# A gated recurrence on the matrix engine: from 64x64 tiles to 64x32 tiles

## The chip, the cores and the metric

The kernel runs as one program on one core of a Trainium2 chip. The metric is device time in microseconds, the median of a few executions. Beside these times there is one profiled execution, whose trace the views below are read from. Engines are named as the profile names them: PE is the matrix engine and PEld its weight loads, DVE, ACT and POOL are the vector, scalar and GpSimd engines, SP is the engine that only issues DMAs here. All data are float32.

## What is computed

The input is `x[8, 32, 256, 256]` (batch, channel, row, column). Four layers follow one another, each adding its result to its input: a Fourier layer, a 5x5 convolution, a gated recurrence over the image's columns, and running maxima in four directions with a 1x1 mix. Only the recurrence is changed. With a column of 256 rows x 32 channels as its state, it is, for each batch and each of 255 columns in turn (cut from the reference):

```
pad = jnp.pad(prev_col, ((0, 0), (1, 1), (0, 0)))
x = jnp.concatenate([pad[:, :-2], pad[:, 1:-1], pad[:, 2:]], axis=-1)
i_vals = jnp.einsum('bhk,ok->bho', x, weight_ih) + bias_ih
h_vals = jnp.einsum('bhc,oc->bho', cur_col, weight_hh) + bias_hh
...
r = jax.nn.sigmoid(r_i + r_h)
z = jax.nn.sigmoid(z_i + z_h)
n = jnp.tanh(n_i + r * n_h)
return n * z + cur_col * (1.0 - z)
```

So each gate (r, z, n) needs three taps of the previous column (the row above, the same row, the row below; 32 channels each) and, called "own" in the kernel, one product of the current input column. For r and z the own part is added into the same sum; for n it stays apart (`nh`), since it is multiplied by r first.

## The kernel before, in words

**Layout.** The 128 partitions hold 4 row classes x 32 channels: partition 32 i + c has the rows h = 4 q + i, and q (64 of them) lies along the free axis. A state tile is `hs[P, 4 batches, 64 + 2]`, with a zero at either end. Two neighbouring classes, 0 and 1 or 2 and 3, form a half ("pair") of 64 partitions. Row h's neighbours are in the classes beside it: for classes 0 and 3 one neighbour lies in the other half and at q - 1 or q + 1.

**Order of the work.** The batch is cut in two chains x = 0 and 1 of four batches each, which take turns: half step n = 2 w + x does column w for chain x. There are 510 half steps with products. Each needs the state of half step n - 2. The order is written out by hand (a manual schedule), every engine takes its instructions in program order.

**Products** (`gates`, `own`, `within`, `across`; lines 736 to 795). A weight tile of 64x64 holds the two classes of one half. `within` (L742) is two matmuls, half to the same half: for a gate it covers the same-row tap and the neighbour inside the half, and with other weights the own part. `across` (L750) is two matmuls from one half to the other, once for the neighbour at the same q (`SAME`) and once for the one at q - 1 or q + 1 (`NEXT`). A half step is so 3 gates x (2 + 2 + 2) plus 3 own x 2 = 24 matmuls of 256 columns each. `gates` writes out their order: r within, z across, ni within, z across, r own of the *next* half step, r across, z within, r across, z own of the next, ni across, nh own of the next, ni across. Explicit waits on a semaphore `tiles` keep matmuls that add into one PSUM tile from different halves apart. PSUM has eight tiles: r, z, nh and ni for either chain.

**Elementwise part** (`step`, L817 to L832). ACT: sigmoid of r (L817), sigmoid of -z (L819) and of z (L820), tanh (L824), and then one piece of `normalise` (L722), which prepares the columns of the next block of eight columns. DVE: (nh + bias) * r (L818), + ni (L823), one piece of other work, * z (L829), + a (L831), which gives the new state. POOL: a = (1 - z) * column (L826) and the residual add (L832). The pieces on DVE are the running maximum (L853) in the half steps of chain 0 and statistics (L864) in those of chain 1.

**Blocks and queues.** A block is eight columns. The input columns `xw` are loaded on SP two blocks ahead (L711); their normalised form `norms[bi]` is one tile per block, two of them in turn, filled a half block of one batch at a time by `normalise`. SP also stores the sums and the running maxima of a block (L842), 16 DMAs of 256 KB each.

Of the kernel before, what the change touches and what calls it, by code (L numbers as in the profile page):

```python
# [9 lines left out]
F32 = mybir.dt.float32  # L10
AF = mybir.ActivationFunctionType
# [5 lines left out]
P = 128  # L17
B, C, H, W = 8, 32, 256, 256
# [5 lines left out]
A = 4  # L24
Q = H // A
# [267 lines left out]
def flat(t):  # L293
    return t.rearrange("p b w q -> p b (w q)")
# [377 lines left out]
def recurrence(tc, k, d, x2d, x3d, fwd, stb, first, loaded, mean1, mv3):  # L672
# [7 lines left out]
    NH = 4  # L680
    NC = 2
    BC = B // NC
    with ExitStack() as ctx:
        one = ctx.enter_context(tc.tile_pool(name="bc", bufs=1))
        blk = ctx.enter_context(tc.tile_pool(name="bb", bufs=2))
# [3 lines left out]
        def rows(i):  # L689
            return slice(32 * i, 32 * i + 32)  # L690
# [12 lines left out]
            nc.vector.memset(t, 0.0)  # L703
        bst = one.tile([P, B, NB, 6], F32, name="bst")

        raws, norms, psums = {}, {}, {}

        def load(bi):
            if bi:
                t = blk.tile([P, B, WB, Q], F32, name=f"xw_{bi}", tag="xw", bufs=4)  # L710
                nc.sync.dma_start(  # L711
                    out=flat(t), in_=x2d[:, :, :, bi * WB : (bi + 1) * WB, :].rearrange("b a c w q -> (a c) b (w q)")
                )
            else:
                t = first
                nc.sync.dma_start(out=flat(t[:, B - 1 : B]), in_=first_columns(x2d, B - 1, B))
            raws[bi] = t
            norms[bi] = blk.tile([P, B, WB, Q], F32, name=f"xn_{bi}", tag="xn")

        def normalise(bi, b, half):  # L720
            w = slice(half * WB // 2, (half + 1) * WB // 2)
            nc.scalar.activation(  # L722
                norms[bi][:, b, w], raws[bi][:, b, w], AF.Identity, bias=shift[:, b : b + 1], scale=sc[:, 1, b : b + 1]
            )

        R, Z, N = 0, 1, 2
        OWN, WITHIN, SAME, NEXT = 1, 0, 2, 3
        pairs = (slice(0, 64), slice(64, 128))


        sem, count = tc.alloc_semaphore("tiles"), [0]
# [8 lines left out]
        def within(out, kind, gate, src, start, stop, wait=None):  # L740
            for i, r in enumerate(pairs):
                ins = nc.tensor.matmul(out[r], lhsT=weights[r, kind, gate, :], rhs=src[r], start=start, stop=stop)  # L742
                if wait and i == 0:
                    ins._wait_ge(sem, wait)

        def across(out, kind, gate, prev, stop, wait=None, signal=False):
            for i, q0 in ((0, 2), (1, 0)):
                r = pairs[i]
                q0 = q0 if kind == NEXT else 1
                ins = nc.tensor.matmul(  # L750
                    out[pairs[1 - i]],
                    lhsT=weights[r, kind, gate, :],
                    rhs=prev[r, :, q0 : q0 + Q],
                    start=False,
                    stop=stop,
                )
                if wait and i == 0:
                    ins._wait_ge(sem, wait)
                if signal and i == 1:
                    ins.then_inc(sem, 1)  # L760
                    count[0] += 1
                    tc.add_to_no_dep_group("signals", ins.ins)
                    tc.no_tile_sem_insts.add(ins.ins.name)
                    some[0] = True

        def own(n, gate):
# [5 lines left out]
            out = psums[n, key] = ps.tile([P, BC, Q], F32, name=f"{key}_{n}", tag=f"{key}{x}")  # L772
            within(out, OWN, gate, norms[w // WB][:, x * BC : (x + 1) * BC, w % WB, :], True, gate == N)

        def gates(n, prev):

            same = prev[:, :, 1 : 1 + Q]
# [12 lines left out]
            across(ni, SAME, N, prev, False, signal=True)  # L792
            own(n + 1, N)
            across(ni, NEXT, N, prev, True)

        def step(w, x):
            bi, wi = w // WB, w % WB
            bs = slice(x * BC, (x + 1) * BC)
            raw, cur = raws[bi][:, bs, wi, :], norms[bi][:, bs, wi, :]
            new = hs[x][w % NH][:, :, 1 : 1 + Q]  # L800
            if w == 0:
                nc.vector.tensor_copy(new, cur)
            else:
                n, prev = NC * w + x, hs[x][(w - 1) % NH]
                if n == NC:
                    for gate in (Z, R, N):
                        own(n, gate)
                    nc.tensor.drain().then_inc(sem, 1)
                    count[0] += 1
# [7 lines left out]
                rs = nc.scalar.activation(r, p["r"], AF.Sigmoid, bias=brz[:, 0:1])  # L817
                nc.vector.scalar_tensor_tensor(m, p["nh"], bhh[:, 2:3], r, ALU.add, ALU.mult)  # L818
# [4 lines left out]
                nc.vector.tensor_tensor(m, p["ni"], m, ALU.add)  # L823
# [5 lines left out]
                ins = nc.vector.tensor_tensor(m, m, z, ALU.mult)  # L829
                tc.add_manual_dep(ins.ins, product.ins.name, AFTER, reason="the sum behind it then need not wait")  # L830
                free(nc.vector.tensor_tensor(new, m, a, ALU.add))  # L831
            nc.gpsimd.tensor_tensor(raw, raw, new, ALU.add)  # L832
# [14 lines left out]
        def running(bi, wi):  # L847
            def piece():
                if wi == 0:
                    tops[bi] = blk.tile([P, B, WB, Q], F32, name=f"fm_{bi}", tag="fm", bufs=2)  # L850
                t, x = tops[bi], raws[bi][:, :, wi]
                last = t[:, :, wi - 1] if wi else tops[bi - 1][:, :, WB - 1] if bi else x
                nc.vector.tensor_tensor(t[:, :, wi], x, last, ALU.max)  # L853
                if wi == WB - 1:
                    store(bi, fwd, t)

            pieces[0].append(piece)
# [323 lines left out]
```

## Time and profile before

| what | value |
|---|---|
| time, median of 3 runs (range) | 3231.57 us (3227.11 to 3237.39) |
| profiled execution, first to last instruction | 3226.3 us |
| granted PE clock, mean over the span | 0.931 |
| PE busy, whole span | 2866.3 us (89%) |
| recurrence, 1160 to 2530 us: PE, DVE, ACT, POOL busy | 1356.41, 1230.82, 1129.28, 705.79 us |
| PE clock granted in the recurrence | 1.00 |

The page gives no time of the profiled execution other than its span; 3226.3 us is 5.3 us, or 0.16%, under the median. A row of groups reads: line, engine, operation, output<-inputs, shapes, count | busy us in all, mean ns of one | idle us of the engine just before them, with what ended it. A float32 matmul appears as two weight loads and two matmul records, called passes below. The recorded end of a matmul is modelled; its start is not, and so spacing is read from starts.

### The profile page before, as it was taken

How to read it: one execution, taken by the hardware profiler on the slowest of the kernel's cores; microseconds unless marked ns; L12 is line 12 of the kernel's file. 1: busy time of each engine (PE TensorE's matmuls, PEld its weight loads, DVE VectorE, ACT ScalarE, POOL GpSimd, SP SyncE). 2: the span in 40 equal slices, each digit the busy share in tenths (PEclk: the TensorE clock that was granted, in tenths of full speed). 3: DMA queues.
4: the chain of work that ended last, by engine and by line, in shares of the span. 5: the costliest groups of instructions: out<-in, count | busy, mean ns of one | idle time of the engine just before them, and what ended most of it. 6: DMA issues, size and time to landing. Idle time of an engine off the chain costs nothing.

```text
span 3226.3 us, 112014 instructions
## 1 busy us (share of the span) xinstructions
PE 2866.3 (89%) x47802; PEld 1666.4 (52%) x47802; DVE 2614.3 (81%) x5188; ACT 1862.5 (58%) x4362; POOL 860.8 (27%) x1241
## 2 busy tenths in 40 slices
PE   7975799999999969999999999999999577777776
PEld 4655344444444446666666666666666233333332
DVE  5742577777767759999999999999999799999998
ACT  3422365565565657888888888888887222222222
POOL 0110011111111145555555555555555200000000
PEclk9985899999999989999999999999999788888998
DMA  9978577888777545665555555666554588878885
GB/s 385 387 288 193 129 187 193 196 194 195 186 182 197 138 110 153 159 159 151 146 148 147 147 146 151 157 159 159 155 143 121 188 306 305 308 311 314 313 308 217
DMA packets 527058, 655.75 MB, mean 203 GB/s; under 512 B 388825, under 2 KB 389737, under 8 KB 500829
## 3 DMA queue, kind: packets, MB, share of 16 engines
q1 hardware_dynamic: 483628, 494.33, 53.9%
q0 software_dynamic: 17200, 85.05, 8.1%
q10 hardware_dynamic: 25728, 69.21, 5.4%
q8 instruction: 374, 6.13, 0.8%
q14 instruction: 128, 1.04, 0.1%
HBM read 371.63 MB, written 272.63 MB: 200 GB/s over the span
## 4 chain that ended last, share of the span: by engine, by line
PE 54%; DVE 25%; DMA 8%; SPq 6%; issue 5%; ACT 2%; POOL 0%; DVEq 0%; ACTq 0%; POOLq 0%
PE r L742 13%; PE z L742 12%; PE ni L742 6%; PE nh L742 6%; DMA x2d<-x 6%; SPq L547 5%; DVE rv L993 5%; PE vp L490 4%; DVE x L527 3%; PE yp L131 3%; DVE dq L1005 2%; DVE m L1009 2%; DVE m L1007 2%; DVE x L1002 2%; DVE m L1008 2%
## 5 line engine op out<-in xcount | busy, mean ns | idle before, releaser
L750 PE MATMUL z<-hs,weights 64*64 64x256 f32 x4080 | 539.4, 382 | 0.0
L750 PE MATMUL r<-hs,weights 64*64 64x256 f32 x4080 | 525.2, 375 | 0.0
L750 PE MATMUL ni<-hs,weights 64*64 64x256 f32 x4080 | 524.9, 375 | 0.0
L832 POOL TENSOR_TENSOR xw<-xw,hs 128x256 f32<-128x256 f32 x496 | 339.5, 684 | 635.6 <-DVE hs L831 635.6
L527 DVE SCALAR_TENSOR_TENSOR x<-vp,r,x 64x512 f32<-64x512 f32 (+2 forms) x640 | 350.8, 563 | 164.6 <-PE vp L490 137.8
L1039 ACT ACTIVATE ot<-o,bres 128x512 f32<-128x512 f32 x256 | 155.4, 690 | 541.5 <-PE o L1023 533.9
L490 PE MATMUL vp<-x,c_conv 64*64 64x384 f32 (+2 forms) x4608 | 457.5, 514 | 0.2
L826 POOL TENSOR_TENSOR a<-zm,xn 128x256 f32<-128x256 f32 x510 | 372.7, 731 | 6.4 <-issue 6.2
L1023 PE MATMUL o<-m,wsc 32*32 32x512 f32 x3072 | 237.1, 830 | 152.9 <-DVE m L1009 106.3
L824 ACT ACTIVATE n<-n,bih 128x256 f32<-128x256 f32 x510 | 260.8, 511 | 184.4 <-DVE n L823 184.4
L490 PEld LDWEIGHTS vp<-x,c_conv 64*64 64x64 f32 x4608 | 238.3, 138 | 234.5 <-issue 128.5
L742 PE MATMUL z<-xn,weights 64*64 64x256 f32 x2040 | 305.3, 376 | 24.2 <-ACT xn L722 24.2
L742 PE MATMUL r<-hs,weights 64*64 64x256 f32 x2040 | 319.0, 389 | 4.4 <-DVE hs L831 3.4
L742 PE MATMUL r<-xn,weights 64*64 64x256 f32 x2040 | 305.6, 376 | 1.0 <-ACT rs L817 1.0
L742 PE MATMUL nh<-xn,weights 64*64 64x256 f32 x2040 | 305.7, 376 | 0.0
L742 PE MATMUL z<-hs,weights 64*64 64x256 f32 x2040 | 305.2, 376 | 0.0
L742 PE MATMUL ni<-hs,weights 64*64 64x256 f32 x2040 | 305.2, 375 | 0.0
L722 ACT ACTIVATE xn<-xw,shift,turned 128x256 f32<-128x256 f32 x496 | 291.9, 589 | 0.0
L750 PEld LDWEIGHTS ni<-hs,weights 64*64 64x64 f32 x4080 | 284.4, 133 | 0.3
L818 DVE SCALAR_TENSOR_TENSOR n<-nh,bhh,rs 128x256 f32<-128x256 f32 x510 | 246.3, 483 | 45.3 <-ACT rs L817 30.7
L750 PEld LDWEIGHTS r<-hs,weights 64*64 64x64 f32 x4080 | 281.1, 131 | 0.2
L817 ACT ACTIVATE rs<-r,brz 128x256 f32<-128x256 f32 x510 | 242.7, 476 | 50.8 <-PE r L750 30.3
(165 smaller groups left out, 6267.2 us busy)
## 6 DMA issues: line engine op xcount, KB each, us to landing
xb<-in_xl_dram POOLq DMA_DIRECT2D x96, 768.0 KB, 6.4
xa<-in_xt_dram SPq DMA_DIRECT2D x64, 1024.0 KB
x<-x3d SPq DMA_DIRECT2D x32, 2048.0 KB
fw<-fwd SPq DMA_DIRECT2D x32, 2048.0 KB
out_dram<-ot ACTq DMA_DIRECT2D x64, 1024.0 KB
xw<-x2d SPq DMA_DIRECT2D x31, 2048.0 KB
fwd<-fm SPq DMA_DIRECT2D x248, 256.0 KB
x3d<-xw SPq DMA_DIRECT2D x248, 256.0 KB
```

The source lines that it names most:

```text
L490: ins = nc.tensor.matmul(vps[bank][to], lhsT=k.conv[r, P : P + 64] if kind == 2 else k.conv[r, o], rhs=pair_of(u, ch, g, lo, hi, (2, 0)[i] ...
L527: nc.vector.scalar_tensor_tensor(x, src[o], r1[rows, g : g + 1], x, ALU.mult, ALU.add, accum_out=s1[rows, 0, n, ch, g : g + 1])
L547: (nc.gpsimd if 2 * u + ch == 2 * n - 1 and p % 2 else nc.sync).dma_start(out=x2d[b, a, c0 : c0 + CH, TS * t + lo : TS * t + hi].rearrange ...
L722: nc.scalar.activation(norms[bi][:, b, w], raws[bi][:, b, w], AF.Identity, bias=shift[:, b : b + 1], scale=sc[:, 1, b : b + 1])
L742: ins = nc.tensor.matmul(out[r], lhsT=weights[r, kind, gate, :], rhs=src[r], start=start, stop=stop)
L750: ins = nc.tensor.matmul(out[pairs[1 - i]], lhsT=weights[r, kind, gate, :], rhs=prev[r, :, q0 : q0 + Q], start=False, stop=stop,)
L817: rs = nc.scalar.activation(r, p["r"], AF.Sigmoid, bias=brz[:, 0:1])
L818: nc.vector.scalar_tensor_tensor(m, p["nh"], bhh[:, 2:3], r, ALU.add, ALU.mult)
L824: nc.scalar.activation(m, m, AF.Tanh, bias=bih[:, 2:3])
L826: product = nc.gpsimd.tensor_tensor(a, zm, cur, ALU.mult)
L832: nc.gpsimd.tensor_tensor(raw, raw, new, ALU.add)
L1023: nc.tensor.matmul(pts[b2][i][32 * j : 32 * j + 32].rearrange("p (w q) -> p w q", q=Q), lhsT=wsc[q, b2, t, :], rhs=src[j][q, b2], start=first,
```

## The change

All products of the recurrence are made in tiles of 64 input partitions x 32 output partitions. For a gate there are two kinds left, each of four matmuls, one for each output class: `near` takes the class's own half (same-row tap and neighbour in the half), `far` takes the other half (for classes 0 and 3 the neighbour at q - 1 or q + 1, for 1 and 2 the one at the same q), with the weights that were there before, cut to 32 output columns. The own parts of r and z are near tiles. The own part of nh is made in far tiles, from `swapped`, a copy of the normalised columns with the two halves of partitions exchanged, and it is issued in two parts of two batches (128 columns) each. A new function `swap` makes the copy with two DMAs on SP for each half block. The normalised columns become one tile for each half block (three in turn) in place of one for a block (two in turn). A drain of PE ahead of the first half step is dropped.

```
-            norms[bi] = blk.tile([P, B, WB, Q], F32, name=f"xn_{bi}", tag="xn")
...
+            if b == 0:
+                norms[bi, half] = blk.tile([P, B, HB, Q], F32, name=f"xn_{bi}_{half}", tag="xn", bufs=3)
...
+        def swap(bi, half):
+
+            t = swapped[bi, half] = blk.tile([P, B, HB, Q], F32, name=f"xs_{bi}_{half}", tag="xs")
+            for i in range(2):
+                nc.sync.dma_start(out=flat(t[pairs[1 - i]]), in_=flat(norms[bi, half][pairs[i]]))
...
+        FAR = ((NEXT, 0), (SAME, 1), (SAME, 1), (NEXT, 2))
+
+        def tiles(out, gate, operand, other, start, stop, cols=slice(0, BC), wait=None, signal=False):
...
+            for j in range(A):
+                r = pairs[1 - j // 2 if other else j // 2]
+                kind, src = operand(j)
+                ins = nc.tensor.matmul(
+                    out[rows(j), cols],
+                    lhsT=weights[r, kind, gate, rows(j % 2)],
+                    rhs=src[r, cols],
+                    start=start,
+                    stop=stop,
+                )
+                if wait is not None and j == 0:
                     ins._wait_ge(sem, wait)
...
+            src = column(swapped if gate == N else norms, w, x)
+            tiles(psums[n, key], gate, lambda j: (OWN, src), gate == N, True, gate == N, cols)
...
-            within(r, WITHIN, R, same, False, False)
-            across(z, SAME, Z, prev, False, wait=count[0], signal=True)
-            first = count[0]
-            within(ni, WITHIN, N, same, True, False)
-            across(z, NEXT, Z, prev, False, signal=True)
+            first = near(r, R, prev, start=False, stop=False, signal=True)
+            second = far(ni, N, prev, start=True, stop=False, signal=True)
+            third = near(z, Z, prev, start=False, stop=False, signal=True)
+            own(n + 1, N, slice(0, BC // 2))
+            far(r, R, prev, start=False, stop=True, wait=first)
             own(n + 1, R)
-            across(r, SAME, R, prev, False, wait=first)
-            within(z, WITHIN, Z, same, False, True, wait=count[0])
-            across(r, NEXT, R, prev, True)
+            own(n + 1, N, slice(BC // 2, BC))
+            near(ni, N, prev, start=False, stop=True, wait=second)
+            far(z, Z, prev, start=False, stop=True, wait=third)
             own(n + 1, Z)
-            across(ni, SAME, N, prev, False, signal=True)
-            own(n + 1, N)
-            across(ni, NEXT, N, prev, True)
...
-                    nc.tensor.drain().then_inc(sem, 1)
-                    count[0] += 1
...
                 for b in range(B):
                     normalise(0, b, half)
+                swap(0, half)
...
                             normalise(bi + 1, b, half)
+                            if b == B - 1:
+                                swap(bi + 1, half)
```

More of the change, by code (lines that the diff above doesn't have):

```diff
@@ L682, in recurrence @@
     BC = B // NC
+    HB = WB // 2
     with ExitStack() as ctx:
@@ L704, in recurrence @@
         bst = one.tile([P, B, NB, 6], F32, name="bst")
-        raws, norms, psums = {}, {}, {}
+        pairs = (slice(0, 64), slice(64, 128))
+        raws, norms, swapped, psums = {}, {}, {}, {}
         def load(bi):
@@ L717, in load, with column @@
             raws[bi] = t
-            norms[bi] = blk.tile([P, B, WB, Q], F32, name=f"xn_{bi}", tag="xn")
         def normalise(bi, b, half):
-            w = slice(half * WB // 2, (half + 1) * WB // 2)
+            w = slice(half * HB, (half + 1) * HB)
+            if b == 0:
+                norms[bi, half] = blk.tile([P, B, HB, Q], F32, name=f"xn_{bi}_{half}", tag="xn", bufs=3)
             nc.scalar.activation(
-                norms[bi][:, b, w], raws[bi][:, b, w], AF.Identity, bias=shift[:, b : b + 1], scale=sc[:, 1, b : b + 1]
-            )
+                norms[bi, half][:, b],
+                raws[bi][:, b, w],
+                AF.Identity,
+                bias=shift[:, b : b + 1],
+                scale=sc[:, 1, b : b + 1],
+            )
+        def swap(bi, half):
+            t = swapped[bi, half] = blk.tile([P, B, HB, Q], F32, name=f"xs_{bi}_{half}", tag="xs")
+            for i in range(2):
+                nc.sync.dma_start(out=flat(t[pairs[1 - i]]), in_=flat(norms[bi, half][pairs[i]]))
+        def column(t, w, x):
+            return t[w // WB, w % WB // HB][:, x * BC : (x + 1) * BC, w % HB, :]
         R, Z, N = 0, 1, 2
         OWN, WITHIN, SAME, NEXT = 1, 0, 2, 3
-        pairs = (slice(0, 64), slice(64, 128))
         sem, count = tc.alloc_semaphore("tiles"), [0]
@@ L737, in free @@
                 tc.declare_no_dep(ins.ins, group="signals", reason="later matmuls of the same half step end last")
[L740 to L749, printed above, removed]
+        FAR = ((NEXT, 0), (SAME, 1), (SAME, 1), (NEXT, 2))
@@ L750, in across @@
+        def tiles(out, gate, operand, other, start, stop, cols=slice(0, BC), wait=None, signal=False):
+            for j in range(A):
+                r = pairs[1 - j // 2 if other else j // 2]
+                kind, src = operand(j)
                 ins = nc.tensor.matmul(
[L751 to L754, printed above, removed]
+                    out[rows(j), cols],
+                    lhsT=weights[r, kind, gate, rows(j % 2)],
+                    rhs=src[r, cols],
+                    start=start,
@@ L755, in across @@
                     stop=stop,
                 )
-                if wait and i == 0:
+                if wait is not None and j == 0:
                     ins._wait_ge(sem, wait)
-                if signal and i == 1:
-                    ins.then_inc(sem, 1)
-                    count[0] += 1
[L762 to L766, printed above, removed]
+            if signal:
+                ins.then_inc(sem, 1)
+                count[0] += 1
+                tc.add_to_no_dep_group("signals", ins.ins)
+                tc.no_tile_sem_insts.add(ins.ins.name)
+                some[0] = True
@@ L768, in own, with near, far, operand @@
+            return count[0]
+        def near(out, gate, prev, **flags):
+            return tiles(out, gate, lambda j: (WITHIN, prev[:, :, 1 : 1 + Q]), False, **flags)
+        def far(out, gate, prev, **flags):
+            def operand(j):
+                kind, q0 = FAR[j]
+                return kind, prev[:, :, q0 : q0 + Q]
+            return tiles(out, gate, operand, True, **flags)
+        def own(n, gate, cols=slice(0, BC)):
             w, x = divmod(n, NC)
@@ L771, in own @@
             key = ("r", "z", "nh")[gate]
-            out = psums[n, key] = ps.tile([P, BC, Q], F32, name=f"{key}_{n}", tag=f"{key}{x}")
-            within(out, OWN, gate, norms[w // WB][:, x * BC : (x + 1) * BC, w % WB, :], True, gate == N)
+            if (n, key) not in psums:
+                psums[n, key] = ps.tile([P, BC, Q], F32, name=f"{key}_{n}", tag=f"{key}{x}")
+            src = column(swapped if gate == N else norms, w, x)
+            tiles(psums[n, key], gate, lambda j: (OWN, src), gate == N, True, gate == N, cols)
         def gates(n, prev):
-            same = prev[:, :, 1 : 1 + Q]
             r, z = psums[n, "r"], psums[n, "z"]
             ni = psums[n, "ni"] = ps.tile([P, BC, Q], F32, name=f"ni_{n}", tag=f"ni{n % NC}")
-            within(r, WITHIN, R, same, False, False)
-            across(z, SAME, Z, prev, False, wait=count[0], signal=True)
-            first = count[0]
-            within(ni, WITHIN, N, same, True, False)
-            across(z, NEXT, Z, prev, False, signal=True)
+            first = near(r, R, prev, start=False, stop=False, signal=True)
[3 more added lines that the diff above has]
+            far(r, R, prev, start=False, stop=True, wait=first)
             own(n + 1, R)
-            across(r, SAME, R, prev, False, wait=first)
-            within(z, WITHIN, Z, same, False, True, wait=count[0])
-            across(r, NEXT, R, prev, True)
+            own(n + 1, N, slice(BC // 2, BC))
+            near(ni, N, prev, start=False, stop=True, wait=second)
+            far(z, Z, prev, start=False, stop=True, wait=third)
             own(n + 1, Z)
-            across(ni, SAME, N, prev, False, signal=True)
-            own(n + 1, N)
-            across(ni, NEXT, N, prev, True)
         def step(w, x):
@@ L798, in step @@
             bs = slice(x * BC, (x + 1) * BC)
-            raw, cur = raws[bi][:, bs, wi, :], norms[bi][:, bs, wi, :]
+            raw, cur = raws[bi][:, bs, wi, :], column(norms, w, x)
             new = hs[x][w % NH][:, :, 1 : 1 + Q]
@@ L807, in step @@
                         own(n, gate)
-                    nc.tensor.drain().then_inc(sem, 1)
-                    count[0] += 1
                 gates(n, prev)
```

## Prediction, made before the changed kernel was run

> **What bounds the kernel now.** I read the sums by stretch first, to see the stage the change is in; then that stage's waits; then its timeline. The stretch holding the recurrence (columns: length; busy us and count of PE, PEld, DVE, ACT, POOL; clock; DMA share; GB/s):
>
> ```profile
> 1160.00:2530.00 1370.00, 1356.41 (x24480) 921.81 (x24480) 1230.82 (x2568) 1129.28 (x2552) 705.79 (x1029) 1.00 0.56 146
> ```
>
> PE is busy nearly throughout at full clock, DVE nine tenths. A half step's length comes from the first and last start of a line that runs once in each:
>
> ```profile
> L818 DVE SCALAR_TENSOR_TENSOR n<-nh,bhh,rs x510: 461/483/488, 1170.1 to 2523.0; 128x256 f32<-128x256 f32 x170
> ```
>
> (2523.0 - 1170.1) / 509 = **2.658 us**. PE has 24 matmuls of two passes on four tiles, 12 passes per tile. Their starts in the trace lie 0.2157 us apart: 12 x 0.2157 = 2.588. So PE stands still for 0.07 us in a half step. The stage's waits (waiter <- whom: us, times, longest) say on what:
>
> ```profile
> PEld r L742 <- DVE hs L831: 110.6, 363, 2.3
> DVE n L818 <- ACT rs L817: 30.7, 130, 6.5
> ACT rs L817 <- PE r L750: 29.8, 141, 0.7
> ```
>
> This is a ring: PE waits for the state, ACT for r, DVE for ACT. PE is the tightest part of it, but how near is the next? DVE over two half steps (start, length):
>
> ```profile
> 1600.18 0.48 DVE L818 SCALAR_TENSOR_TENSOR n<-nh,bhh,rs 128x256 f32<-128x256 f32 x1
> 1600.77 0.42 DVE L823 TENSOR_TENSOR n<-ni,n 128x256 f32<-128x256 f32 x1
> 1601.11 0.68 DVE L864 BATCH_NORM_STATS2 bst<-xw 128x6 f32<-128x512 f32 x1
> 1601.84 0.43 DVE L829 TENSOR_TENSOR n<-n,zs 128x256 f32<-128x256 f32 x1
> 1602.30 0.42 DVE L831 TENSOR_TENSOR hs<-n,a 128x256 f32<-128x256 f32 x1
> 1602.91 0.48 DVE L818 SCALAR_TENSOR_TENSOR n<-nh,bhh,rs 128x256 f32<-128x256 f32 x1 [0.19 <-ACT rs L817]
> 1603.50 0.42 DVE L823 TENSOR_TENSOR n<-ni,n 128x256 f32<-128x256 f32 x1
> 1603.84 0.89 DVE L853 TENSOR_TENSOR fm<-xw,fm 128x512 f32<-128x512 f32 x1
> 1604.65 0.41 DVE L829 TENSOR_TENSOR n<-n,zs 128x256 f32<-128x256 f32 x1
> 1605.10 0.42 DVE L831 TENSOR_TENSOR hs<-n,a 128x256 f32<-128x256 f32 x1
> ```
>
> Read the starts. In the lower half step DVE never pauses: the maximum (L853) fills the time until L829. In the upper one it waits for tanh and, at its end, for r. DVE is the near second.
>
> **What the Trainium skill says.** TensorEngine Tiling (Array Packing), Tiling Modes: 64x32 gives eight independent tiles, 64x64 four. The trace agrees, in another stage with exactly these tiles and float32, at twice the columns (start, length):
>
> ```profile
> 335.87 1.95 PE L424 MATMUL up<-tt,c_gw 64*32 64x512 f32 x32
> ```
>
> The 32 passes start in four groups of eight; within a group 7 ns apart, groups 429 ns apart when running. Eight tiles are truly at work, each at 2 x 214.5 ns for twice the columns. PSUM — Partial Sum Buffer, PSUM bank collisions: two row tiles may not write one bank and quadrant at once. Hence the waits of far on near; no trace shows a collision. TensorE: Matmul & The Clock Gate, HAM oscillation: long idle gaps (over some 3.4 us) lower the clock. The trace agrees so far: a stretch with PE busy 12.68 of 17.00 us (2805 to 2822) was still granted 1.00.
>
> **The change, part by part.**
>
> *Products.* Near tiles: r, ni, z and two own parts, 5 matmuls or 10 passes each. Far tiles: ni, r, z and nh, 4 matmuls, 8 passes' worth. At 0.2157 us the longer queue is **10 x 0.2157 = 2.16 us** in place of 2.59. Can a pass hold 0.2157 with 256 columns? Weight loads must hide behind it. A row half now loads 4 x 32 columns in a pass, before 2 x 64: the same. And L131 (128x32 tiles, 256 columns, four loads of the same rows per pass) starts its groups 216 ns apart. A first group of L424 was followed 24 ns late (453 for 429), so I bound the pass at 0.214 to 0.240 (0.216 + 0.024) and take 0.216. Issuing 160 PE instructions a half step doesn't limit either, since the 32x32 stage (L1023) starts a load, a matmul and another load every 16.7 ns (5.6 ns each, 0.89 us for 160).
>
> The two 128-column parts of nh have passes of 107 ns, about one weight load (L424: 103 to 106 ns recorded), so they may take up to some 30 ns more each, 4 x 0.03 = 0.12 us. At 0 or at 0.12 they lie in the far tiles' spare 2 x 0.216 = 0.43 us.
>
> *When each sum is ready*, from the first near r: near r and far ni end at 0.43; half of nh at 0.65; far r waits for near r's signal. PE's end to the start of the waiting sigmoid is 0.3 us in the trace (r's last pass ends at 1.78, L817 starts at 2.05 to 2.09), so far r starts at 0.65 to 0.75, ends by 1.2: **sigmoid of r at 1.5 in place of 2.07**. Behind the waiting far r stand own r and all that follows; near tiles are busy with near z until 0.86, so at most its issue is delayed. Near ni and far z end by 1.8 to 2.0; their waits are long satisfied. z's sigmoid then comes 0.4 to 0.6 us behind r's where it was 0.37 behind; the start of a (L826) is what could feel it.
>
> *The same chain's ring*: state to PE 0.06, PE 1.5, sigmoid to the end of L831 3.07 to 3.17 (L817 starts at 2.05 and 2.09, L831 ends at 5.12 and 5.26): 4.68 us for two half steps, 2.34 each. So neither PE (2.16) nor this ring (2.34) binds; DVE and ACT are late next.
>
> *DVE's ring*, by smallest spacings of starts. L818 to L823 0.59. L823 to L829: 1.07 with statistics (tanh 0.46 later, 0.51 long, 0.10 to react), 1.18 mean with the maximum (mean 908 ns). L829 to L831 0.45, L831 to the next L818 0.34. Sums: **2.46 and 2.56, mean 2.51**. ACT's ring, with the sigmoid of r behind `normalise`: L817 to L818 0.51, to L823 0.59, to tanh 0.46, to L722 0.42, to the next L817 0.49, sum 2.47. POOL: state of n - 1 to a 0.71, a 0.73, reaction 0.11: 1.55 to L829, where DVE needs about 1.58; it fits, barely. I take **2.53**, 0.02 over the DVE ring for this crowding.
>
> *Swap.* Two DMAs of 512 KB a half block, 31 + 1 blocks: 64 MB from SBUF to SBUF. Deadline: about eight half steps, 20 us, after the last piece of `normalise`. DMA: Bandwidth & Descriptors, Anatomy of one DMA, gives 2.0 us plus bytes / 436 GB/s; an estimate from it is 4.4 us for 1 MB. No run yet shows this copy; the nearest row, xf<-xb (128 KB, 8.1 us to landing), bounds it at 8 to 16 us in a crowd. DMA is at 0.56 here, so I charge nothing; the cover is the 20 us, and beyond it every late us is paid. On SP, the swap stands ahead of the column load (due half a block later) and of a block's stores, which wait for POOL's last sum anyway; nothing else is moved past it. Later landing of stores meets no reader before the next stage.
>
> *Start.* Half step 2's own nh now waits for the first swap: eight pieces (8 x 0.5 = 4 us after 1159.2), then 4.4 to 8 us, against the first products at 1161.3 and gates at 1164.2 before. The first sigmoid followed a 1.28-us table load, at 1169.5. PE is in order, so the gates shift to about 1168 to 1171: I charge 3 us (0 to 7). New waits of `normalise` for its buffer are on readers a half step old: nothing. The dropped drain: nothing.
>
> *Sum.* 510 x (2.658 - 2.53) = 65 less 3 = 62 us. Against the span: 3226.3 - 62 = 3164; against the median, 5.3 above it: **3169 us**, -1.9%. With 2.50 (maximum as short as 0.85) it is 3155 with 3 us of start charged; with 2.56, 3185.
>
> **Rivals.**
> - *Half the gain*: only chain 1's half steps shrink, or POOL and the later z hold L829 up. Chain 0's are at 2.61 already, 2.59 the commonest; for it speaks POOL's margin of 0.03. With 2.61 overall: 510 x 0.048 - 3 = 21, 3210 us.
> - *The bound was elsewhere, no change*: the ring closes at 2.65 through DVE's and ACT's order. Against: DVE waits for ACT 30.7 us and ACT for PE 29.8. 3231 us.
> - *Slower: weight loads come out from behind the passes.* Eight tiles must be reloaded within 214 ns; L424 has twice that. If a load of 103 ns were fully exposed, a pass is 0.317, PE 10 x 0.317 = 3.17: +0.51 x 510 = 261 us, 3493. It decides above a pass of 0.266, where PE alone takes today's 2.66. Against it: L131 at 216, and loads starting 7 ns apart.
>
> **Chances.** Main case 0.60, half the gain 0.17, no change 0.07, slower 0.16. About 0.3% (10 us) is what a measurement tells from none. Faster: 0.60 + 0.17 = 0.77; same 0.07; slower 0.16. The range 3148 to 3225 takes in the main case's bounds and the half gain, and leaves out the slower case and part of no change.
>
> **What would show it.** Half step 2.53; sigmoid of r some 1.9 us after the first near r or held by ACT, no longer by PE; PE pass starts 0.216 apart in groups of up to eight, PE idle 0.3 us a half step waiting for the state; DVE idle ahead of L818 nearly gone; swap landing within 20 us. Wrong if passes are over 0.25 apart, if the clock falls below 1.00, or if PE waits for the swap.

## The result, and the profile after

| what | before | changed kernel |
|---|---|---|
| time, median (range), side by side on one chip | 3229.34 us (3225.89 to 3237.39) | 3499.81 us (3494.88 to 3505.63) |
| ratio to before, 95% interval | | 1.0832 [1.0811, 1.0853] |
| profiled span | 3226.3 us | 3496.1 us |
| first (nh + bias) * r to last | 1170.1 to 2523.0 us | 1182.4 to 2792.8 us |

The change makes the kernel 8.3% slower, where 1.9% faster was forecast. All but some 3 us of the difference lies in the recurrence: its first piece of `normalise` starts at 1159.2 us before and at 1162.6 in the changed kernel, and after the last new state the two take another 700.8 and 700.7 us. The stretch of the recurrence in the changed kernel (columns as before):

```profile
1170.00:2800.00 1630.00, 1294.90 (x40776) 906.13 (x40776) 1245.98 (x2562) 1097.99 (x2539) 722.82 (x1028) 0.96 0.64 164
```

PE is busy in four fifths of it and no longer nearly throughout, so PE isn't just slow at its work; it stands still. The clock is 0.96 in place of 1.00. The half step, from the line that runs once in each:

```profile
L841 DVE SCALAR_TENSOR_TENSOR n<-nh,bhh,rs x510: 475/478/488, 1182.4 to 2792.8; 128x256 f32<-128x256 f32 x170
```

(2792.8 - 1182.4) / 509 = **3.164 us** in place of 2.658 and of the forecast 2.53. With the start 12.3 us later, 12.3 + 509 x 0.506 = 269.9 us: the whole difference of the spans (269.8). What does PE stand still for? The waits of the changed kernel (waiter <- whom: us, times, longest):

```profile
PEld r L764 <- DVE hs L854: 197.8, 293, 3.9
ACT rs L840 <- PE r L764: 170.6, 127, 5.6
DVE n L841 <- ACT rs L840: 164.8, 120, 15.4
...
PEld z L764 <- issue: 113.7, 99, 4.9
...
PEld r L764 <- issue: 85.3, 67, 5.1
PE z L764 <- issue: 79.8, 53, 4.4
...
PEld ni L764 <- issue: 77.9, 46, 4.4
```

The first line is the expected one: PE ahead of the state. The last four are new: "issue" is time in which the engine waited for nothing that the profile shows. One of these standstills in PE's timeline:

```profile
1700.42 0.40 PE L764 MATMUL r<-xn,weights 64*32 64x256 f32 x4
1700.49 0.40 PE L764 MATMUL nh<-xs,weights 64*32 64x128 f32 x8
1702.24 0.42 PE L764 MATMUL ni<-hs,weights 64*32 64x256 f32 x4 [1.35 <-issue]
1702.27 0.42 PE L764 MATMUL z<-hs,weights 64*32 64x256 f32 x4
1702.48 0.40 PE L764 MATMUL ni<-hs,weights 64*32 64x256 f32 x4
```

Read the starts: in the middle of a half step, with its state long there, PE starts nothing from about 1700.6 to 1702.24. On either side the groups of passes are 0.21 to 0.24 us apart, as forecast. The chains behind PE (ACT for PE, DVE for ACT) wait with it.

The clue is the place. I numbered PE's instructions through the trace (loads, passes and the few that only handle semaphores). Of the changed kernel's 390 gaps of over 0.45 us between starts in the recurrence, 176 stand behind the very same record of each run of 256; they hold 324 us. What follows them is a load or a pass of r, z, ni and nh alike, so the place is one of the stream, not of the half step. (Of the other 214, with 150 us, 213 end at a weight load for the product of the state with r, as in the first of the waits above.) The recurrence before has no gap at that place, and nine elsewhere. And the page's DMA queues have a row with just that step. Before:

```profile
q8 instruction: 374, 6.13, 0.8%
```

The changed kernel:

```profile
q8 instruction: 504, 8.26, 0.9%
```

(packets, MB, share.) A packet has 16,384 bytes. PE has 95,604 loads and passes before and 128,228 after, with the others 95,817 and 129,007 instructions; by 256 these are 374.3 and 503.9. So q8 brings PE its own instructions, 64 bytes each, 256 to a packet. This is **theory F** (F for fetch): PE runs out of instructions, since a packet waits in the DMA engines behind data, and with 160 instructions a half step 256 of them are used up sooner.

Its numbers in the trace: a packet takes 0.96 us (median); after a standstill PE goes on 1.4 us after it has landed (median; mostly 1.2 to 1.6). In the standstill above the packet starts at 1699.80 and lands at 1700.82, and PE goes on at 1702.24. The packet's *waiting* I count from PE's passing of the common place (two records behind it) to the packet's start. One may wait, before PE notices, the time of 256 instructions less 0.96 and 1.4: before, 256 / 96 x 2.658 = 7.1, so 4.7 us; after, undisturbed, 256 / 160 x 2.63 = 4.2, so **1.85 us**. Packets of the changed kernel, by waiting:

| waiting, us | packets | followed by a standstill at the common place |
|---|---|---|
| under 1.5 | 116 | 2 |
| 1.5 to 2.0 | 35 | 17 |
| 2.0 to 2.5 | 31 | 26 |
| over 2.5 | 137 | 131 |

In the kernel before none of the recurrence's 191 packets is followed by one; the longest waiting there was 4.4 us, short of 4.7.

### The profile page after: what moved, and what is told of

The parts are those of the page before. It is cut to its first block, busy times and chain, and to the rows that moved or that the text cites. A ratio compares the mean times of both kernels' runs of the same rounds, so it can differ in the third digit from the quotient of the medians.

```text
span 3496.1 us, 146027 instructions
## 1 busy us (share of the span) xinstructions
PE 2807.8 (80%) x64114; PEld 1648.8 (47%) x64114; DVE 2631.4 (75%) x5188; ACT 1835.7 (53%) x4362; POOL 879.2 (25%) x1241
## 4 chain that ended last, share of the span: by engine, by line
DVE 35%; PE 33%; issue 14%; DMA 8%; SPq 5%; ACT 3%; POOL 1%; DVEq 0%; ACTq 0%; POOLq 0%
PE r L764 6%; PE z L764 6%; PE vp L490 6%; DVE rv L1019 4%; SPq L547 4%; DMA x2d<-x 4%; PE ni L764 3%; DVE n L852 3%; DVE hs L854 3%; DVE x L527 3%; PE up L424 3%; DVE n L841 2%; PE yp L131 2%; DVE n L846 2%; DVE dq L1031 2%
## 5 line engine op out<-in xcount | busy, mean ns | idle before, releaser
L764 PE MATMUL r<-hs,weights 64*32 64x256 f32 x8160 | 725.5, 398 | 104.5 <-DVE hs L854 51.2
L764 PE MATMUL z<-hs,weights 64*32 64x256 f32 x8160 | 729.1, 391 | 48.1 <-issue 47.7
L764 PE MATMUL ni<-hs,weights 64*32 64x256 f32 x8160 | 717.9, 395 | 60.8 <-issue 60.6
L764 PE MATMUL nh<-xs,weights 64*32 64x128 f32 (+1 forms) x8152 | 475.7, 280 | 60.2 <-issue 47.4
L764 PE MATMUL z<-xn,weights 64*32 64x256 f32 x4080 | 366.1, 390 | 61.3 <-issue 32.1
L764 PE MATMUL r<-xn,weights 64*32 64x256 f32 x4080 | 364.7, 392 | 19.7 <-issue 17.6
L764 PEld LDWEIGHTS z<-hs,weights 64*32 64x32 f32 x8160 | 302.7, 109 | 105.7 <-issue 70.6
L842 ACT ACTIVATE zm<-z,brz 128x256 f32<-128x256 f32 x510 | 239.1, 469 | 196.0 <-PE z L764 149.5
L764 PEld LDWEIGHTS nh<-xs,weights 64*32 64x32 f32 x8152 | 291.8, 108 | 93.6 <-issue 59.2
L764 PEld LDWEIGHTS ni<-hs,weights 64*32 64x32 f32 x8160 | 260.5, 108 | 84.1 <-issue 77.9
```

Of the source, the lines that this page charges most:

```text
L764: ins = nc.tensor.matmul(out[rows(j), cols], lhsT=weights[r, kind, gate, rows(j % 2)], rhs=src[r, cols], start=start, stop=stop,)
```

## The experiments

Theory F is as above. Its rivals are told in the expectations, by letters; those in all of them: the swap's traffic, the number or the shape of the matmuls by itself, and, for a part of the loss, contention of VectorE and GpSimd. "Standstills" below are gaps of over 0.45 us at the common place. "Undisturbed" is the median half step away from gaps, for chain 0 / chain 1.

| run | PE instructions a half step | packet waiting, mean us | standstills: number, us | half step: undisturbed; mean, us | ratio to before |
|---|---|---|---|---|---|
| before | 96 | 1.24 | 0 | 2.59 / 2.72; 2.658 | |
| changed kernel | 160 | 2.30 | 176, 324 | 2.81 / 2.46; 3.164 | 1.0832 |
| e1_swap_alone | 96 | 2.16 | 0 | 2.59 / 2.73; 2.663 | 1.0017 |
| e2_no_swap | 160 | 1.72 | 86, 168 | 2.82 / 2.45; 3.061 | 1.056 |
| e3_nh_whole | 144 | 2.38 | 133, 216 | 2.80 / 2.46; 2.983 | 1.0506 |
| e4_mixed_tiles | 108 | (not counted) | 0 | 4.32 / 4.32; 4.324 | 1.2663 |
| e5_spread_traffic | 160 | 2.23 | 187, 291 | 2.81 / 2.46; 3.043 | 1.0616 |
| e6_vector_product | 160 | 2.34 | 171, 333 | 2.65 / 2.46; 3.146 | 1.0816 |
| e7_160_in_64x64 | 160 | 1.72 | 80, 119 | 2.62 / 2.66; 2.971 | 1.0511 |
| e8_three_together | 144 | 2.31 | 143, 192 | 2.66 / 2.46; 2.824 | 1.0263 |
| e9_paced_traffic | 160 | 2.14 | 171, 248 | 2.80 / 2.46; 2.989 | 1.0521 |
| e10_few_stores | 160 | 1.78 | 90, 178 | 2.80 / 2.46; 2.949 | (other work) |
| e11_paced_whole_vector | 144 | 2.12 | 121, 141 | 2.65 / 2.46; 2.766 | 1.0198 |
| e12_paced_no_swap | 144 | 1.35 | 4, 2.5 | 2.65 / 2.52; 2.616 | 0.9939 |

### e1: the swap without the tiles

The kernel before, with norms in half blocks and the swap's copies, which nothing reads.

```
+                swap(0, half)
...
+                            if b == B - 1:
+                                swap(bi + 1, half)
```

> The 64x64 products of before, with the normalised columns in half-block tiles and the swapped copy made by the same two DMAs a half block, which nothing reads. PE has 96 instructions a half step. Theory F (PE starves for instructions: its program is fetched 256 instructions, 16 KB, at a time, and a fetch that queues behind data comes late when 256 instructions last only 4 us): 256 instructions last 7.1 us here, so later fetches still arrive in time; 3230 to 3255 us, few PE stalls. Rival D (the 64 MB of swap traffic is the cost, whatever the number of instructions): 3400 us or more. Rival W (waits or tile shape): about 3230.

Measured: 3234.12 us against 3229.18, 1.0017 [1.0009, 1.0026], as F had it; D is out. The copies and the smaller tiles of norms cost some 5 us. But see the packets' waiting: it rises from 1.24 to 2.16 us, nearly to that of the changed kernel, and not one standstill follows, for with 96 instructions a half step 4.7 us are to spare. The limit itself can be seen here: of 191 packets four waited longer than 4.7 us (4.77, 4.95, 4.98 and 5.21), and behind these four alone PE pauses at the common place, by 0.22, 0.25, 0.33 and 0.42 us. Traffic alone isn't the cause; it needs the denser instruction stream.

### e2: the tiles without the swap

The changed kernel, nh's own part in near tiles from the columns themselves.

```
-            src = column(swapped if gate == N else norms, w, x)
-            tiles(psums[n, key], gate, lambda j: (OWN, src), gate == N, True, gate == N, cols)
+            src = column(norms, w, x)
+            tiles(psums[n, key], gate, lambda j: (OWN, src), False, True, gate == N, cols)
...
-                swap(0, half)
```

> The changed kernel with nh's own part made in near tiles from the normalised columns themselves, and no swap. PE still has 160 instructions a half step, the near tiles have 12 passes (2.59 us). Theory F: stalls at every 256 instructions remain, a little shorter since the DMA queues are emptier; half step 2.9 to 3.1 us, 3350 to 3460 us. Rival D (swap traffic): the loss goes, 3230 to 3250 us. A second rival, that PE waits for the swapped copy, expects the same 3230 to 3250.

Measured: 3407.28 us, 1.056 [1.0507, 1.0613], within F's range; D and the wait for the copy are out. Two thirds of the loss stay. The packets wait 0.6 us less, and the standstills are halved (86, 168 us). Both halves of F are seen here: 160 instructions are enough for standstills, less traffic gives fewer.

### e3: 144 instructions in place of 160

The changed kernel with nh's own part in one piece of 256 columns.

```
-            own(n + 1, N, slice(0, BC // 2))
...
-            own(n + 1, N, slice(BC // 2, BC))
+            own(n + 1, N)
```

> The changed kernel with nh's own part in one piece of 256 columns in place of two of 128: 144 PE instructions a half step instead of 160, no other change. Theory F: 256 instructions last a tenth longer (4.5 us for 4.05), so stalls shrink: 3400 to 3465 us. A rival in which 64x32 tiles or DMA traffic cost by themselves: within 20 us of 3500.

Measured: 3390.28 us, 1.0506 [1.049, 1.0521]: the same arithmetic and the same bytes of data in 10% fewer instructions, and 110 us less (10 us more than F's range allowed). The packets wait as long as in the changed kernel (2.38 us); the time of 256 instructions grows to 256 / 144 x 2.63 = 4.7 us, the spare to 2.3, and standstills now begin at a waiting of 2.0 to 2.5 us (2 of 24 packets at 1.5 to 2.0, 16 of 35 at 2.0 to 2.5).

### e4: fewer instructions by mixing tile sizes

The changed kernel with near and own products in 64x64 tiles, far ones in 64x32 (27 matmuls; the last half of a signalling or waiting product stays in 64x32).

```
-            return tiles(out, gate, lambda j: (WITHIN, prev[:, :, 1 : 1 + Q]), False, **flags)
+            return wide(out, gate, WITHIN, prev[:, :, 1 : 1 + Q], False, **flags)
```

> The changed kernel with the near and own products in 64x64 tiles again (two matmuls, three where a signal or a wait needs the upper half in two tiles) and only the far products in 64x32 tiles: 108 PE instructions a half step, passes per tile as in the changed kernel (10 near, 8 far), the swap kept. Theory F: 256 instructions last 6.2 us, stalls nearly gone; half step about 2.63 (2.46 with statistics, 2.80 with the running maximum, which POOL slows), 3215 to 3245 us. If a change of tile size drains PE (the skill's tiling page says so), each of some ten changes a half step costs up to 0.2 us: over 4000 us. Rival D: about 3500.

Measured: 4086.72 us, 1.2663 [1.2642, 1.2684], with no standstill at all (256 instructions last 10.2 us). Another cost took their place: F's time was missed by over 800 us, and the time is that of the drains. PE's timeline in e4:

```profile
1700.22 0.42 PE L764 MATMUL r<-hs,weights 64*32 64x256 f32 x4
1700.45 0.38 PE L785 MATMUL z<-hs,weights 64*32 64x256 f32 x2
1700.46 0.40 PE L764 MATMUL r<-hs,weights 64*32 64x256 f32 x4
1700.79 0.43 PE L785 MATMUL r<-xn,weights 64*64 64x256 f32 x2
1700.80 0.43 PE L785 MATMUL nh<-xs,weights 64*64 64x256 f32 x2
1701.05 0.38 PE L785 MATMUL r<-xn,weights 64*64 64x256 f32 x2
```

From the last 64*32 group to the first 64*64 one it is 0.33 us, within a size 0.22 to 0.26. The Trainium skill, TensorEngine Tiling (Array Packing), Key Properties, says that a change of tile mode drains the engine, and the trace agrees: at the six changes of a half step the groups of passes lie 0.32 us apart in the mean, within a size 0.24, so a change costs some 0.08 us. The drains are the smaller part: six times 0.08 is 0.5 us. The larger is that near and far, of different sizes, no longer run side by side: the trace has 16 groups of passes a half step one after another, and 16 x 0.24 + 0.5 = 4.3 us (measured 4.32; 2.16 was reckoned for two queues). As a test of F by its time this run is worth little.

### e5: the traffic spread, first try

The changed kernel; stores and column loads cut to 256 KB pieces and issued two a half step.

```
+                        if wi == 0 and x == 1:
...
+                        for _ in range(2):
+                            if late and (wi or x):
+                                late.pop(0)()
```

> The changed kernel with the same bytes in the recurrence, but its stores and the load of the next columns are issued two 256 KB pieces a half step over the whole block instead of in bursts at the block's start and middle. Theory F (TensorE stands still because the 16 KB packets that bring its instructions wait behind the data of the stores, the loads and the swap): the waiting time of these packets, mean 2.2 us in the changed kernel, falls below 1.5 us, most of the 175 standstills and their 333 us go, and the time falls to 3200 to 3330 us. Rival C (the standstills come from the number of instructions alone, for which the fetch is too slow whatever else moves): their number stays within a third of 175 and the time within 3430 to 3520 us.

Measured: 3432.89 us, 1.0616 [1.0595, 1.0636]; 187 standstills. By its numbers the expectation of C was met. But the edit didn't do what it said, as SP's queue in e5 shows:

```profile
1505.63 0.69 SPq L716 DMA_DIRECT2D xw<-x2d  x1
1516.57 1.11 SPq L742 DMA_DIRECT2D xs<-xn  x2
1519.08 0.49 SPq L871 DMA_DIRECT2D fwd<-fm  x1
1519.66 1.93 SPq L871 DMA_DIRECT2D x3d<-xw  x1
1521.69 1.34 SPq L716 DMA_DIRECT2D xw<-x2d  x1
```

SP stands at the swap until its columns are there (nothing is issued from 1506.3 to 1516.57), and then issues all that follows it in the program, since those pieces wait for nothing. Two bursts a block, as before. Where an instruction stands in a program doesn't set its time; what it waits for does. The run decides nothing on C.

### e6: the running maximum without GpSimd beside it

Undisturbed half steps of chain 0 take 2.81 us, where DVE's ring was forecast at 2.56. DVE and then POOL in the changed kernel:

```profile
1529.47 0.48 DVE L841 SCALAR_TENSOR_TENSOR n<-nh,bhh,rs 128x256 f32<-128x256 f32 x1
1530.05 0.42 DVE L846 TENSOR_TENSOR n<-ni,n 128x256 f32<-128x256 f32 x1
1530.39 1.17 DVE L876 TENSOR_TENSOR fm<-xw,fm 128x512 f32<-128x512 f32 x1
1531.49 0.41 DVE L852 TENSOR_TENSOR n<-n,zs 128x256 f32<-128x256 f32 x1
```

```profile
1530.28 0.74 POOL L849 TENSOR_TENSOR a<-zm,xn 128x256 f32<-128x256 f32 x1
```

The maximum takes 1.17 us with POOL's product a whole beside it; before the change, where z comes earlier and a overlaps it in part, 0.89. In e6 DVE makes the product a itself in chain 0.

```
-                product = nc.gpsimd.tensor_tensor(a, zm, cur, ALU.mult)
+                product = nc.gpsimd.tensor_tensor(a, zm, cur, ALU.mult) if x else None
...
+                if not x:
+                    nc.vector.tensor_tensor(a, zm, cur, ALU.mult)
```

> The changed kernel with the product a taken from GpSimd to VectorE in the half steps of chain 0, those with the running maximum; chain 1 is left alone. Theory V (GpSimd's product and VectorE's maximum slow each other, 680 ns becoming 1171 ns): the maximum is back at about 0.68 us and undisturbed half steps of chain 0 go from 2.80 to 2.80 - 0.49 + 0.34 = 2.65 us; the standstills stay, so the whole time falls by 20 to 60 us only. Rival M (the maximum is slow for its own sake, or because of DMA traffic): it stays near 1.17 us, the half step grows to about 3.1 us and the kernel loses some 60 us more.

The maximum in e6 (least, median, most ns):

```profile
L879 DVE TENSOR_TENSOR fm<-xw,fm x248: 676/683/694, 1228.3 to 2785.4; 128x512 f32<-128x512 f32 x124
```

It is back at 0.68 us and the undisturbed half step of chain 0 at 2.65, as V had it to 0.01. The Trainium skill, SBUF — State Buffer, SBUF: two separate sides, says that VectorE operations with two SBUF inputs and GpSimd operations that read SBUF hold one port pair exclusively. The trace agrees in kind and nearly in size: shut out until a's end at 1531.02 and then 0.68 long, the maximum would end at 1531.70; it ended at 1531.56.

But the time, 3497.13 us, is the changed kernel's (1.0816 [1.0784, 1.0848]); the 20 to 60 us foretold of V didn't come. Standstills are as many (171, 333 us), the mean half step fell by only 0.018 us. I read it so, without a run for it: while packets set the pace, a faster DVE only has PE reach the missing instructions earlier.

### e7: 160 instructions in the old tiles

The kernel before, in 64x64 tiles and without a swap, most matmuls cut into two of 128 columns.

```
+        parts = (slice(0, BC // 2), slice(BC // 2, BC))
...
-                ins = nc.tensor.matmul(out[r], lhsT=weights[r, kind, gate, :], rhs=src[r], start=start, stop=stop)
+                    ins = nc.tensor.matmul(
+                        out[r, c], lhsT=weights[r, kind, gate, :], rhs=src[r, c], start=start, stop=stop and (start or c == cuts[-1])
+                    )
```

> The kernel before, its 64x64 tiles, order and DMA traffic, with most of its products cut into two halves of 128 columns, so that TensorE has 160 instructions a half step as in the changed kernel; no swap. Theory F: standstills that lie a multiple of 256 instructions apart appear here too, some 50 to 150 of them, 100 to 250 us in sum, and the time is 3300 to 3480 us. Rival S (what costs time is the shape of the 64x32 tiles, not the count): no such standstills, and the time is below 3260 us, or above it only by weight loads that show as passes longer than half of 0.2157 us, without a common place in the instruction stream.

Measured: 3399.05 us, 1.0511 [1.0488, 1.0535]. The standstills of the changed kernel appear in the old tiles, at the same place of 256: 80 of them, 119 us. Of 189 packets that waited under 2.0 us none is followed by one, of 71 over 2.5 us 68 are. The fair comparison is e2, which also has 160 instructions and no swap, in the new tiles: 86 standstills and 3407 us. For the standstills the size of the tiles isn't what matters, the number of instructions is. One part of this time is its own: undisturbed half steps of chain 1 spread up to 3.5 us, and I didn't follow that further.

### e8: three edits together

nh in one piece, e5's spreading, e6's product on DVE.

> The changed kernel with three edits: nh in one piece (144 instructions a half step), stores and loads spread over the block, and the product a on VectorE in chain 0. If F and V are both right the standstills nearly go and half steps take about (2.65 + 2.46) / 2 = 2.55 us: 3226 - 509 x 0.11 + 12 = some 3185 us, and 3185 to 3260 us with a few standstills left, that is within 1.5% of the kernel before on either side. If F is wrong the standstills stay at 130 and 230 us and the time is near 3350 us.

Measured: 3317.28 us, 1.0263 [1.0237, 1.0289], between the two numbers: V's part came (2.66 / 2.46 undisturbed), the standstills stayed at 143 and 192 us, as they must with e5's bursts.

### e9: the traffic spread and held back

e5, and each piece waits for the residual sum of its half step.

```
-                                late.pop(0)()
+                                issued = late.pop(0)()
+                                tc.add_manual_dep(issued.ins, beat.ins.name, AFTER, reason="one half step at a time")
```

> As e5_spread_traffic, but each 256 KB piece also waits for the POOL addition of its own half step, so that SyncE can't issue a block's pieces in two bursts behind the swaps, as it did there. Theory F: with the traffic even over the block the waiting time of the instruction packets is below 1.5 us in nearly every half step of the block instead of 3 us after the swaps, the standstills fall from 187 to below 90, and the time to 3250 to 3380 us. Rival C (the fetch is too slow for 160 instructions a half step whatever moves beside it): 150 or more standstills and 3400 us or more.

Measured: 3396.45 us, 1.0521 [1.0494, 1.0548]: 103 us less than the changed kernel, but neither expectation whole. By half step of the block the packets' waiting, which in the changed kernel goes from 0.8 us where nothing moves to 3.8, is now 1.6 to 2.1 us in most, and still 2.7 to 3.3 in those behind the two swaps of a block; the mean fell only from 2.30 to 2.14. The standstills became shorter, not fewer: 171, 248 us. Spread evenly, most packets wait close to the 1.85 us that decide.

### e10: an eighth of the stores

The changed kernel, storing inside the recurrence one column of a block's eight. Whole blocks are stored only after the recurrence, all from the last block's tiles, so that the values of the earlier blocks are left out of its result; only its recurrence is compared.

```
-        def store(bi, dst, t):
+        def store(bi, dst, t, n=Q):
...
-                        out=dst[bi, :, a, b2].rearrange("(i c) n -> c i n", c=C),
-                        in_=t[rows(a), 4 * b2 : 4 * b2 + 4].rearrange("p i w q -> p i (w q)"),
+                        out=dst[bi, :, a, b2].rearrange("(i c) n -> c i n", c=C)[:, :, 0:n],
+                        in_=t[rows(a), 4 * b2 : 4 * b2 + 4].rearrange("p i w q -> p i (w q)")[:, :, 0:n],
```

> The changed kernel, but inside the recurrence only an eighth of each stored column block is written, and whole blocks are written once the recurrence has ended, all with the last block's values; so the recurrence moves 3.5 MB less a block, and the end of the kernel some 128 MB more. Only the recurrence's half steps are compared. Theory F: the waiting time of the instruction packets falls below 1.4 us, the standstills from 175 to below 60, and the mean half step from 3.16 us to 2.65 to 2.85 us. Rival C: more than 130 standstills stay, and the mean stays above 3.0 us. The kernel's own time is longer by the stores at its end, some 400 to 600 us.

Measured: mean half step 2.949 us, 90 standstills, 178 us (the kernel itself 3934.99 us, with the stores at its end). Neither expectation is met (F had under 60 standstills and at most 2.85 us, C over 130 and over 3.0), and it is the place in the block that tells. In the five half steps of a block in which the stores used to move (the fourth to the eighth), the changed kernel has 85 standstills and 116 us, e10 has 6 and 4 us. In the half steps behind the swaps and the load, which e10 leaves alone, they stay. Where the data goes, the standstills go.

### e11 and e12: towards a version without standstills

e11 is e8 with e9's pacing. e12 is e11 without the swap (e2's edit, nh in one piece).

> e8_three_together with its pieces paced as in e9_paced_traffic: nh in one piece (144 instructions a half step), traffic even over the block, the product a on VectorE in chain 0. Theory F with V: of 141 standstills and 201 us some 30 and 50 us are left, the half step is 2.56 to 2.66 us, and the time 3190 to 3240 us, level with the kernel before or up to 1.2% faster. Rival C: 120 or more standstills and 3300 us.

> e11_paced_whole_vector without the swap: nh's own product in the same rows as those of r and z, from the columns themselves, in one piece (144 instructions a half step). In e9 to e11 the longest waits of the instruction packets, 2.7 to 3.5 us, and half of the standstills are left in the half steps that follow a swap and the load. Theory F: without the swap the longest waits go too; of 120 standstills and 152 us some 20 to 60 and 20 to 80 us are left, the half step is 2.58 to 2.68 us, and the time 3190 to 3245 us, about level with the kernel before. Rival: the near tiles, with seven products against five in the far ones, become the bound (each product two passes of 0.2157 us, 7 x 2 x 0.2157 = 3.02 us a half step if near and far can't be shared out): then undisturbed half steps are 3.0 us and the time 3400 us.

e11: 3290.73 us, 1.0198 [1.0175, 1.022]; 121 standstills and 141 us where F was given 30 and 50. By its numbers this is rival C's result (120 or more, 3300 us). But the standstills and the longest waits are again most frequent behind the swaps, which I had taken too lightly. e12 takes them away, with the same 144 instructions and the same pacing, and that C can't explain: 3207.37 us against 3227.49, **0.9939 [0.9928, 0.9951]**, 0.6% faster than the kernel before. Its recurrence, its half steps and its packets:

```profile
1165.00:2510.00 1345.00, 1329.87 (x36680) 916.91 (x36672) 1231.46 (x2819) 1072.75 (x2542) 541.14 (x775) 1.00 0.58 148
```

```profile
L845 DVE SCALAR_TENSOR_TENSOR n<-nh,bhh,rs x510: 467/477/486, 1170.0 to 2501.3; 128x256 f32<-128x256 f32 x170
```

```profile
q8 instruction: 472, 7.73, 1.0%
```

The clock is 1.00 again, PE busy throughout, the half step (2501.3 - 1170.0) / 509 = 2.616 us. Packets wait 1.35 us in the mean, 2.88 at most; 256 / 144 x 2.59 = 4.6 us leaves 2.24 to spare, and of 287 packets 4 are followed by a standstill, all of which had waited over 2.5 us; F had allowed 20 to 60. The rival of seven near products (3.02 us) fell: chain 1's half step rose by 0.07 us only.

## Why the prediction was wrong, point by point

- **The step that failed** is the sentence "Issuing 160 PE instructions a half step doesn't limit either". It was read from a stage that *starts* a load, a matmul and a load every 16.7 ns, and that is the speed once PE has its instructions. The supply of these instructions is another resource: packets of 256 on a queue that the page had listed (q8, 374 packets) and the prediction didn't read. It wasn't in the working at all. It costs, against undisturbed half steps of 2.63 us in the mean, 509 x (3.164 - 2.63) = 272 us. (The 324 us of standstills are more, presumably since DVE catches up a part of each.) The profile before had the sign on show, in a stage ahead of the recurrence. From its chain of work that ended last (start, us, what):

```profile
228.14 3.64 PE mp L269 x128
231.78 3.11 issue
...
241.13 3.63 PE mp L269 x127
244.76 2.89 issue
```

Some 128 passes with as many loads are 256 instructions, used up in 3.6 us; then PE stands still on "issue". That stage of the kernel before has ten such standstills, 22 us, all at the same common place, and in each PE goes on 1.3 to 1.5 us after a packet has landed.

- **Products, 10 x 0.2157 us**: right within the bounds given. Groups of one product lie 0.22 to 0.24 us apart (1702.24 and 1702.48 above), and the forecast condition "wrong if passes are over 0.25 apart" didn't occur. The slower rival named 3493 us, close to the measured time, but by exposed weight loads, which the trace doesn't show in this kernel: right number, wrong mechanism, and so no support for it.
- **DVE's ring**: 2.46 with statistics was right (2.456 undisturbed in chain 1). With the maximum it was 2.56 and measured 2.81: the term mis-sized is the 1.18 us from L823 to L829, taken from a mean in which POOL's product overlapped the maximum by half. The change moves z later, a with it, and now it overlaps whole: 1.43 us. The prediction named the later a, as a worry for the wait on a, not for the shared port. So without any standstill the gain would have been 509 x (2.658 - 2.63) = 14 us, about what the late start took away.
- **Swap, charged nothing**: 5 us by itself with its smaller tiles (e1), and in the changed kernel, together with the column load behind it, the longest packet waits of a block. "DMA is at 0.56 here, so I charge nothing" asked whether the swap would land in time, not who would wait behind it.
- **Start, 3 us (0 to 7)**: 12.3 us, of which 3.4 us lie ahead of the recurrence. The other 8.9 us are the wait for the first copy: from the first piece of `normalise` to the first (nh + bias) * r it takes 19.8 us where it took 10.9; in the other kernels that read the copy it is 17.0 to 21.3, in those without a swap 10.8 to 11.1. The copy is issued at 1166.7 and nh's first pass starts at 1175.1, 8.4 us later, just over the 4.4 to 8 us taken. (The 4.4 came from a formula that its page gives for DMAs issued by GpSimd; these are issued by SP.)
- **Clock**: that it would stay at 1.00 was wrong, 0.96. In e12, nearly without standstills, it is 1.00. The trace's record of the clock has 31 stretches at half clock in the recurrence, 126 us in all. One begins within 3.5 us of the end of each of the nine standstills over 4 us, and none so near any of the 78 shorter than 1.5 us. So the lower clock comes with the long standstills and isn't what makes PE stand still. Passes lost at most 63 us by it; how much of that PE would have had to wait anyway is left open.
- **The chances**: slower at 0.16 was one mechanism. Two thirds more instructions on PE could meet a limit that no row of the page prices, and that was a reason for more.

## What to carry to other kernels

When an edit multiplies the instructions of an engine, price their supply: packets of the instruction queue, the time in which 256 are used up, less 0.96 us for the packet and 1.4 us to go on, against how long packets wait in that stage's traffic. In these kernels 4.2 us per 256 was not enough, nor 4.6 to 4.7 us beside swaps; 4.6 us with even traffic and no swap was, but for four short standstills. A gap on "issue" in the middle of work whose inputs are there is the sign; count where in the stream it falls. And to spread DMAs over time give each something to wait for: order alone lets an idle queue run ahead.

## What of the hardware was not expected

- PE's instructions come in 16,384-byte packets of 256 on a DMA queue (374 packets for 95,817 instructions, 504 for 129,007), and these wait longer where more data moves; PE's common place of standing still was the same in all eleven kernels that had standstills in the recurrence.
- PE went on some 1.4 us after a late packet had landed, and the limit that follows from it was sharp: in e1, where 4.7 us were to spare, only the four packets that waited 4.77 us or more were followed by a pause.
- A packet's mean waiting: 1.24 us in the kernel before, 1.35 with paced stores and loads and no swap (e12), 2.1 to 2.4 with the swaps and all stores.
- VectorE's maximum of 128x512: 0.68 us alone, 1.17 with a GpSimd product of 0.74 us beside it; batch statistics of the same size stayed at 0.68 beside the same product (kernel before).
- A change between 64x64 and 64x32 tiles cost some 0.08 us each time (e4).
